# A graph layer on one core: the final gathers without iotas between them, the final part's first loads taken out of the final part, and one PSUM pool kept to the end

## The chip, the core and the metric

The kernel runs on one core of one Trainium2 chip. The core has five engines that work side by side, each through its own list of instructions in a fixed order: TensorE (PE, with its weight loads as PEld), VectorE (DVE), ScalarE (ACT), GpSimd (POOL) and SyncE (SP), which here only starts transfers. Data moves between memory and the core by DMA transfers, which an engine starts and which then run by themselves; an engine waits for another one, or for a transfer, by semaphores. The metric is the device time of one execution in microseconds (us); less is better.

## What is computed

The reference, cut to what matters (6,250 nodes, 100,000 edges sorted by `dst`, rows of 256 numbers):

```python
theta_x = (x[dst] - x[src]) @ theta_w.T + theta_b
phi_x = x[src] @ phi_w.T + phi_b
e = relu(theta_x + phi_x)
out = segment_max(e, dst, num_segments=6250)      # 0 where a node has no edge
return layernorm(x + where(isfinite(out), out, 0))
```

An edge's value is a part that hangs on `dst` alone, A = x theta^T + biases, plus a part that hangs on `src` alone, B = x (phi - theta)^T. So the maximum over a node's edges is relu(A of the node + the maximum of B over its sources), and the kernel looks for that maximum of B.

## The kernel before

**Stages.** The first 618 nodes ("the first part") are done by running maxima along sorted edges. The other 5,632 nodes are 44 tiles of 128. For these, B is cut into 17 slots of up to 383 rows. For each slot and node at most one source row is fetched, by a product with a one-hot matrix on PE (`slot_halves`, the matmuls of L1172; ACT and DVE make the one-hot tiles `hot` from row numbers `want`, which SP loads, L1207), and DVE takes the running maximum into `acc` (L1186). The edges that no slot has taken stand in a list of 257 steps, 256 of which are gathered: 33 groups of up to 8 steps, each step one indirect gather of 128 rows of `b_rows` on POOL (`gather_2`, L540) and one running maximum on DVE (L709). Each group's result is stored to `maxima_2` in memory (L1701; the last ones two steps at a time, L1748, and the last single step, L724). The slots' products and the list run side by side, from about 243 us to 605 us; this is called the list stage below.

**The final part** handles the 44 tiles in shares of 8, 8, 8, 4, 4, 4, 4, 2 and 2 tiles (`last_shares`, `rows_of`), and each share in pieces of two tiles (22 pieces). POOL gathers for each tile the rows of `maxima_2` that hold its nodes' list results (`gather` in `rows_of`, `g<-maxima,place`, 44 gathers; none can be issued before the last store of the list has landed). For a piece PE adds the bias (L1466), multiplies the transposed columns of x, `kept`, with theta (L1469), and transposes `acc` (L1478). DVE takes the maximum of gathered rows and `acc` (L1479), adds A (L1480), and adds relu of that to x with a sum along the row (L1483). Then comes the normalisation of the share, piecemeal between the next pieces: squares on ACT (L1512), the inverse root on DVE (L435 to L441), scaling on ACT (L1527; in the late shares half of it on DVE, L1523) and the store of the share by SP (L1533; the last by ACT, L1507).

**Rings and what they make wait.** x tiles (8 tiles of rows, 1 MB) stand in `x_ring` with 4 buffers; in the list stage the biases and the first part have used these. The transposed columns (4 tiles, 0.5 MB) stand in `kept_ring` with 3 buffers. Gathered rows have 6 buffers. A load into a used buffer waits for its last reader, which for an x tile is the store of the finished share.

**Order.** The program below is written in one order; a scheduler then lays down a fixed list for each engine, in which an instruction may be put ahead of others written before it if it is free to go. `behind_in_order` keeps an instruction behind a named one in that list. Before the change the x and `kept` loads of the final part are kept behind the last load of `want` in this way. SP's list is worked off strictly in order: an SP instruction that waits holds up all behind it.

**Iotas.** `gather` issues, while `paused[0]` is set, a small iota into a tile that nobody reads behind each gather (L508). It is set for a part of the first gathers and again for the final 44.

**PSUM.** 8 banks: `ps_misc` has two tiles of one bank, `ps_fetch` three of two banks (`ps_f`). In the final part a piece takes one bank for A and one for the transposed `acc`: at first by turns from `ps_misc` and from halves of `ps_f` (`by_turns`); once the last slot's work has been issued, `ps_fetch` is closed and a pool `ps_end` of six one-bank tiles (`ps_e`) opened in its place.

Of the kernel before, what the change touches and what calls it, by code (L numbers as in the profile page):

```python
# [39 lines left out]
FP = mybir.dt.float32  # L40
# [8 lines left out]
PSUM = bass.MemoryType.PSUM  # L49
DRAM = bass.MemoryType.DRAM  # L50

P = 128
BIG2 = 3.0e38
EPS = 1e-5
STEPS = 8
# [3 lines left out]
EARLY_SHARES = 12  # L59
# [19 lines left out]
RUNS_BEHIND = 3  # L79
# [3 lines left out]
X_AHEAD = 4  # L83
WANTS = 3
X_RING = 4
LAST_CHUNKS = 5
HALVES_AT_ONCE = 6
SPREAD_FROM = 9
# [5 lines left out]
LIST_GROUPS = (LIST + STEPS - 1) // STEPS  # L94
# [350 lines left out]
def gnn_kernel(ctx: ExitStack, tc: tile.TileContext, x, src, dst, theta_w, theta_b, phi_w, phi_b, out):  # L445
    nc = tc.nc
    N, D = x.shape
    E = src.shape[0]
    T = -(-E // P)
    KC = D // P  # L450
# [4 lines left out]
    NT1 = Q1 + 1  # L455
# [18 lines left out]
    body = ctx.enter_context(ExitStack())  # L474
# [3 lines left out]
    x_columns = dram.tile([P, TILES * KC * P], FP, name="x_columns")  # L478
# [19 lines left out]
    def node_rows(t, part, j0, n):  # L498
        if (part, j0, n) == LAST:
            return t[P * Q1 : N1, :].rearrange("p (o d) -> p o d", o=1)  # L500
        base, tiles = (0, Q1) if part == 1 else (N1, TILES)
        return flat(t, (base + j0) * D, [[tiles * D, P], [D, n], [1, D]])

    def present(t, part, j0, n):
        return t[: LEFT1 if (part, j0, n) == LAST else P, :n, :]
# [14 lines left out]
    def behind_in_order(one, name, reason):  # L520
        after = mybir.DependencyInfo(mybir.DependencyClass.NoSync, mybir.DependencyReason.DATA)
        tc.add_manual_dep(one.ins, name, after, reason=reason)
# [14 lines left out]
    paused = [False]  # L537
# [143 lines left out]
    one = nc.vector.tensor_copy(ids_1[:, : T1 + 2], dst_1)  # L681
# [740 lines left out]


    x_tiles, m_tiles = {}, {}
    def rows_of(part, j0, n, ps_tile):


        share = part, j0, n
        at = j0 % STEPS if part == 2 else 0
        if at == 0:  # L1430
            x_tiles[part] = x_ring.tile([P, STEPS, D], FP, name="x_f")
            rows = x_ring.tile([P, STEPS, D], FP, name="x_f") if part == 1 else gathered.tile([P, STEPS, D], FP, name="g")
            m_tiles[part] = rows
        x_f = x_tiles[part][:, at : at + n, :]
        if share == LAST:
            nc.vector.memset(x_f[:, 0, :], 0.0)
        one = nc.sync.dma_start(present(x_f, *share), node_rows(x, *share))
        if part == 2:
            behind_in_order(one, latest_codes[0], "chosen codes ahead of x")
        m = m_tiles[part][:, at : at + n, :]  # L1440
        maxima, places = (maxima_1, place_1) if part == 1 else (maxima_2, place_2)
        for k in range(n):
            gather(m[:, k, :], maxima, places[:, j0 + k : j0 + k + 1])
        totals = work.tile([P, STEPS], FP, name="totals", bufs=4)

        def piece(k):
            w = min(2, n - k)
            if part == 2:
                j = j0 + k
                if j % 4 == 0:  # L1450
                    x_tiles[0] = kept_ring.tile([P, 4 * KC, P], FP, name="kept")
                    rows = x_columns[:, j * KC * P : (j + 4) * KC * P]
                    one = nc.sync.dma_start(x_tiles[0], rows.rearrange("p (j n) -> p j n", n=P))
                    behind_in_order(one, latest_codes[0], "chosen codes ahead of the final rows")
                x_t = x_tiles[0][:, j % 4 * KC :]
            else:
                ps = ps_tile().rearrange("p (i n) -> p i n", i=4)
                for i in range(w):
                    for c in range(KC):
                        nc.tensor.transpose(ps[:, 2 * i + c, :], x_f[:, k + i, c * P : (c + 1) * P], ident)  # L1460
                x_t = work.tile([P, 4, P], FP, name="x_t")
                nc.scalar.copy(x_t[:, : 2 * w], ps[:, : 2 * w])
            yield
            a = ps_tile().rearrange("p (i d) -> p i d", i=2)
            bias_of = bias_terms.rearrange("p (o d) -> p o d", o=1)
            nc.tensor.matmul(a[:, :w, :], pick, bias_of.to_broadcast([P, w, D]), start=True, stop=False)  # L1466
            for i in range(w):
                for c in range(KC):
                    nc.tensor.matmul(  # L1469
                        a[:, i, :], x_t[:, 2 * i + c, :], weights[:, c, :], start=False, stop=(i == w - 1 and c == KC - 1)  # L1470
                    )
            some = m[:, k : k + w, :]
            if part == 2:
                ps = ps_tile().rearrange("p (i d) -> p i d", i=2)
                for i in range(w):
                    at = (j0 + k + i) * P
                    for c in range(KC):
                        nc.tensor.transpose(ps[:, i, c * P : (c + 1) * P], acc[:, c, at : at + P], ident)  # L1478
                nc.vector.tensor_tensor(some, some, ps[:, :w, :], op=ALU.max)  # L1479
            nc.vector.tensor_tensor(some, some, a[:, :w, :], op=ALU.add)  # L1480
            for i in range(k, k + w):
                y = x_f[:, i, :]
                one = nc.vector.scalar_tensor_tensor(  # L1483
                    y, m[:, i, :], 0.0, y, op0=ALU.max, op1=ALU.add, accum_out=totals[:, i : i + 1]
                )
                used.append(one.ins.name)
            yield

        return [piece(k) for k in range(0, n, 2)], normalise(part, j0, n, x_f, totals)
# [215 lines left out]
        while halves_left[0] > max(2 * LAST_CHUNKS, 2 * LAST_CHUNKS + halves_ahead * (1.0 - done)):  # L1705
            fetch_half()

    assert len(runs_left) == RUNS_BEHIND and RUNS_BEHIND + 1 + NT1 < EARLY_SHARES
    for i in range(LIST_GROUPS):
        if i == len(runs_left):  # L1710
            chunk_heads()
# [29 lines left out]
            add_up(n_bad, flags)  # L1741
        if i >= EARLY_SHARES:
            next(early_shares, None)
    next(heads, None)
    for i in range(LIST_GROUPS - LEAD, LIST_GROUPS - 1):
        for k in range(0, STEPS, 2):
# [5 lines left out]
    left = LIST - (LIST_GROUPS - 1) * STEPS  # L1752
    run(2, lists[-1], left, caps_2, (LIST_GROUPS - 1) * STEPS, carried_2t, (), carry_row)
    list_done[0] = latest_run[0]
    paused[0] = True
    for _ in range(HALVES_AT_ONCE):
        fetch_half()
    for _ in early_shares:
# [7 lines left out]
    def by_turns():  # L1766

        given[0] += 1
        if given[0] % 4 in (1, 2):
            return misc()  # L1770
        if not halves_of_tile:
            both = ps_fetch.tile([P, CW], FP, name="ps_f")
            halves_of_tile.extend([both[:, : 2 * D], both[:, 2 * D :]])
        return halves_of_tile.pop(0)

    fetch_open, pieces_done = [True], [0]

    def half_between():
        pieces_done[0] += 1
# [2 lines left out]

    at_end = Shares(by_turns)
    for share in last_shares:
        if not parts and begun[0] is None and fetch_open[0]:
            at_end.step()
            fetch_open[0] = False
            fetch.close()
            ps_end = body.enter_context(tc.tile_pool(name="ps_end", bufs=6, space=PSUM))
            at_end.ps_tile = lambda: ps_end.tile([P, 2 * D], FP, name="ps_e")  # L1790
        at_end.add(*share, between=half_between)
    assert not parts and not fetch_open[0]
    at_end.finish()


    body.close()
# [33 lines left out]
```

## Time and profile before

| | |
|---|---|
| median of 3 runs | 688.44 us (686.49 to 690.26) |
| the profiled execution's own time | 683.69 us |
| its span in the trace | 681.8 us |
| busy: PE / DVE / ACT / POOL | 633.4 / 623.5 / 491.3 / 471.8 us |
| share of the span | 93% / 91% / 72% / 69% |
| mean granted clock of PE | 0.981 |
| moved by DMA | 168.21 MB, 247 GB/s on average |

Shares over the whole span mix stages with different limits, so what the final part is worth is read from that part: which engine's or transfer's wait ends last there. A row of a timeline has a start (us from the start of the span), a length, the engine, the line of the kernel and the operation; in brackets stands how long the engine had been idle before and what ended that. Rows of SPq are starts of transfers by SP, not the transfers. The page gives the costs of the operations over the whole span as a mean; for single stages the timeline and tables by window are used.

### The profile page before, as it was taken

The numbers are of one execution on the slowest core, as the hardware profiler recorded it, in microseconds if no ns is written. First come the engines' busy times: TensorE is split into PE (matmuls) and PEld (weight loads), VectorE is DVE, ScalarE is ACT, GpSimd is POOL, SyncE is SP. The second block draws the span as 40 slices with busy tenths as digits, with TensorE's granted clock in tenths as the row PEclk, the third lists the DMA queues.
The fourth block names the chain that finished last, engine by engine and source line by source line (L and its number), as shares of the span: only waits on it lengthen the run. The fifth ranks groups of instructions, "written<-read, shape, count | busy, mean of one in ns | idle before, by whom it ended". The sixth has DMA issues, their size and how long they took to land.

```text
span 681.8 us, 9602 instructions
## 1 busy us (share of the span) xinstructions
PE 633.4 (93%) x2860; PEld 520.2 (76%) x2860; DVE 623.5 (91%) x1208; ACT 491.3 (72%) x678; POOL 471.8 (69%) x515
## 2 busy tenths in 40 slices
PE   4998889799999899999999999999999999998990
PEld 3887768687888688788888887888877777787880
DVE  6899999999999999999999999989998998767886
ACT  1554557989898577798696979786869786713775
POOL 7101288999992876777777777777777777468880
PEclk9999989999999899999999999999999999998995
DMA  7897644555655687778787989888788887895975
GB/s 238 304 340 282 224 127 138 149 169 189 208 171 189 201 279 263 256 231 270 239 297 220 305 289 272 271 262 271 255 266 283 266 285 261 279 365 178 321 262 193
DMA packets 61849, 168.21 MB, mean 247 GB/s; under 512 B 11926, under 2 KB 21950, under 8 KB 55774
## 3 DMA queue, kind: packets, MB, share of 16 engines
q1 hardware_dynamic: 40482, 107.92, 46.2%
q0 software_dynamic: 19040, 52.50, 26.3%
q10 hardware_dynamic: 2268, 7.11, 2.7%
q8 instruction: 24, 0.39, 0.2%
q14 instruction: 35, 0.29, 0.2%
HBM read 104.25 MB, written 63.23 MB: 246 GB/s over the span
## 4 chain that ended last, share of the span: by engine, by line
PE 40%; DVE 23%; DMA 16%; issue 10%; POOL 5%; ACT 4%; DVEq 0%; ACTq 0%; POOLq 0%; SPq 0%
PE ps_f L1172 34%; DMA g<-b_rows,list_src 8%; DVE acc L1186 4%; DVE g L709 4%; POOL g L540 4%; PE ps_b L793 3%; DMA want<-chosen_rows 2%; DVE hot L1219 2%; DMA g<-maxima,place 2%; DVE work L1354 2%; ACT hot L1221 1%; DMA out_dram<-x_f 1%; ACT x_f L1527 1%; DMA b_rows<-b_sb 1%; DVE g L1479 1%
## 5 line engine op out<-in xcount | busy, mean ns | idle before, releaser
L1172 PE MATMUL ps_f<-hot,terms 128*128 128x512 f32 x2112 | 491.5, 393 | 12.3 <-DVE acc L1186 10.2
L1172 PEld LDWEIGHTS ps_f<-hot,terms 128*128 128x128 f32 x2112 | 396.1, 189 | 101.2 <-DVE acc L1186 14.4
L540 POOL DMA_INDIRECT g<-b_rows,list_src x256 | 263.6, 1030 | 81.3 <-issue 46.8
L1221 ACT ACTIVATE hot<-want,minus_row 128x1024 fp32r<-128x1024 f16 (+1 forms) x201 | 207.9, 1070 | 77.9 <-PE ps_f L1172 76.1
L1186 DVE TENSOR_TENSOR acc<-acc,ps_f 128x1024 f32<-128x1024 f32 (+1 forms) x192 | 216.1, 1129 | 9.6 <-PE ps_f L1172 9.2
L1225 ACT ACTIVATE hot<-hot 128x1024 fp32r<-128x1024 f32 (+1 forms) x201 | 187.4, 974 | 0.9
L709 DVE SCALAR_TENSOR_TENSOR g<-g,caps 128x256 f32<-128x256 f32 x334 | 160.4, 483 | 15.3 <-DMA g<-b_rows,list_src 13.3
L540 POOL DMA_INDIRECT g<-b_rows,src x72 | 105.3, 1462 | 28.3 <-issue 14.4
L1219 DVE TENSOR_SCALAR hot<-want,row_id 128x1024 fp32r<-128x1024 f16 (+1 forms) x93 | 67.0, 724 | 3.5 <-DMA want<-chosen_rows 2.3
L793 PE MATMUL ps_b<-weights_b,x_t 128*128 128x256 f32 x228 | 53.2, 387 | 3.8 <-ACT x_t L781 3.5
L540 POOL DMA_INDIRECT g<-maxima,place x44 | 43.2, 982 | 17.9 <-DMA maxima<-g 10.9
L793 PEld LDWEIGHTS ps_b<-weights_b,x_t 128*128 128x128 f32 x228 | 42.9, 193 | 11.1 <-ACT x_t L781 5.6
L1512 ACT ACTIVATE squares<-x_f,r 128x256 bf16<-128x256 f32 x47 | 23.1, 493 | 19.5 <-DVE r L1509 19.5
L1469 PE MATMUL ps_e<-weights,kept 128*128 128x256 f32 x144 | 35.2, 388 | 0.0
L796 ACT COPY b_sb<-ps_b 128x512 f32<-128x512 f32 (+1 forms) x25 | 14.4, 577 | 24.8 <-PE ps_b L793 20.6
L1469 PEld LDWEIGHTS ps_e<-weights,kept 128*128 128x128 f32 x144 | 28.3, 197 | 4.0
L508 POOL IOTA pause<- 128x160 f32 x92 | 28.2, 306 | 0.6
L1527 ACT ACTIVATE x_f<-x_f,r 128x256 f32<-128x256 f32 x40 | 20.7, 587 | 10.5 <-DVE r L1519 10.5
L1003 POOL MEMSET work<- 128x1584 f32 x1 | 2.3, 2256 | 33.7 <-ACT b_sb L796 33.7
L781 ACT COPY x_t<-ps_xt 128x512 f32<-128x512 f32 (+1 forms) x29 | 16.2, 585 | 9.1 <-PE ps_xt L777 7.8
L1479 DVE TENSOR_TENSOR g<-g,ps_e 128x512 f32<-128x512 f32 x18 | 12.4, 688 | 7.4 <-DMA g<-maxima,place 3.3
L1184 ACT COPY acc<-ps_f 128x1024 f32<-128x1024 f32 (+1 forms) x12 | 11.2, 938 | 10.9 <-PE ps_f L1172 6.3
(288 smaller groups left out, 457.6 us busy)
## 6 DMA issues: line engine op xcount, KB each, us to landing
maxima<-g SPq DMA_DIRECT2D x41, 1024.0 KB
want<-chosen_rows SPq DMA_DIRECT2D x89, 256.0 KB
x_q<-in_x_dram SPq DMA_DIRECT2D x12, 512.0 KB
b_rows<-b_sb ACTq DMA_DIRECT2D x12, 512.0 KB
x_columns<-x_t SPq DMA_DIRECT2D x22, 256.0 KB
kept<-x_columns SPq DMA_DIRECT2D x11, 512.0 KB
raw<-b_rows SPq DMA_DIRECT2D x16, 256.0 KB
g<-b_rows,list_src POOLq DMA_INDIRECT x256, 5.0
```

The lines of the kernel that those rows point to most:

```text
L508: return nc.gpsimd.iota(t, pattern=[[step, t.shape[1]]], base=base, channel_multiplier=per_partition, allow_small_or_imprecise_dtypes=True,)
L540: one = nc.gpsimd.indirect_dma_start(out=to, out_offset=None, in_=table, in_offset=bass.IndirectOffsetOnAxis(ap=offsets, axis=0))
L709: one = nc.vector.scalar_tensor_tensor(g[:, k, :], last[part], caps[:, t : t + 1], g[:, k, :], op0=ALU.min, op1=ALU.max)
L793: nc.tensor.matmul(ps[:, h, :], x_t[:, h, k, :], weights_b[:, k, :], start=(k == 0), stop=(k == KC - 1))
L1172: one = nc.tensor.matmul(ps[:, w : w + 512], terms[:, part, b, h * P : (h + 1) * P], hot[b][:, w : w + 512], start=(i == 0), stop=(i == n ...
L1186: one = nc.vector.tensor_tensor(to, to, ps, op=ALU.max)
L1219: nc.vector.tensor_scalar(hot[b], want, row_id[:, b : b + 1], None, op0=ALU.is_equal)
L1221: one = nc.scalar.activation(hot[b], want, AF.Abs, bias=minus_row[:, b : b + 1], scale=1.0)
L1225: nc.scalar.activation(apart, apart.bitcast(FP), AF.Relu, bias=1.0, scale=-1.0)
L1469: nc.tensor.matmul(a[:, i, :], x_t[:, 2 * i + c, :], weights[:, c, :], start=False, stop=(i == w - 1 and c == KC - 1))
L1512: nc.scalar.activation(squares, x_f[:, k, :], AF.Square, bias=mean[:, k : k + 1], scale=1.0, accum_out=var[:, k : k + 1])
L1527: nc.scalar.activation(x_f[:, k, :], x_f[:, k, :], AF.Identity, bias=mean[:, k : k + 1], scale=inv[:, k : k + 1])
```

## The change

Three edits, all on the way from the list stage into the final part:

1. `paused[0] = True` ahead of the final part goes, so the 44 final gathers are issued with no iota behind them.
2. A new function `load_ahead` loads the first four x tiles (`X_TILES_AHEAD`) and the first three `kept` tiles (`KEPT_AHEAD`). It is written into the loop over the list groups, one call for each group from the 29th on (`AHEAD_FROM = 28`). These loads are not kept behind the loads of `want`. The final part takes these tiles instead of loading them.
3. `ps_fetch` is kept open to the end. Once no slot's work is left, `by_turns` gives two of eight tiles from `ps_misc` and six as halves of `ps_f`; `ps_end` is gone.

```diff
+X_TILES_AHEAD = 4
+KEPT_AHEAD = 3
+AHEAD_FROM = 28
...
+    def load_ahead(i):
+        if i < X_TILES_AHEAD:
+            x_f = x_ring.tile([P, STEPS, D], FP, name="x_f")
+            share = 2, i * STEPS, STEPS
+            nc.sync.dma_start(present(x_f, *share), node_rows(x, *share))
+            x_ahead.append(x_f)
+        if i < KEPT_AHEAD:
+            kept_ahead.append(load_kept(i * 4)[0])
+    def load_kept(j):
+        tile_of = kept_ring.tile([P, 4 * KC, P], FP, name="kept")
+        rows = x_columns[:, j * KC * P : (j + 4) * KC * P]
+        return tile_of, nc.sync.dma_start(tile_of, rows.rearrange("p (j n) -> p j n", n=P))
...
-            x_tiles[part] = x_ring.tile([P, STEPS, D], FP, name="x_f")
+            if part == 2 and x_ahead:
+                x_tiles[part] = x_ahead.pop(0)
+            else:
+                x_tiles[part] = x_ring.tile([P, STEPS, D], FP, name="x_f")
...
-        one = nc.sync.dma_start(present(x_f, *share), node_rows(x, *share))
-        if part == 2:
-            behind_in_order(one, latest_codes[0], "chosen codes ahead of x")
+        if part == 1 or j0 // STEPS >= X_TILES_AHEAD:
+            one = nc.sync.dma_start(present(x_f, *share), node_rows(x, *share))
+            if part == 2:
+                behind_in_order(one, latest_codes[0], "chosen codes ahead of x")
...
+        if i >= AHEAD_FROM:
+            load_ahead(i - AHEAD_FROM)
...
-    paused[0] = True
...
-        if given[0] % 4 in (1, 2):
+        every = 4 if halves_left[0] or begun[0] is not None else 8
+        if given[0] % every in (1, 2):
             return misc()
...
-        if not parts and begun[0] is None and fetch_open[0]:
-            at_end.step()
-            fetch_open[0] = False
-            fetch.close()
-            ps_end = body.enter_context(tc.tile_pool(name="ps_end", bufs=6, space=PSUM))
-            at_end.ps_tile = lambda: ps_end.tile([P, 2 * D], FP, name="ps_e")
         at_end.add(*share, between=half_between)
...
     at_end.finish()
+    fetch.close()
```

What stands in the lists of the engines now, at three places. (Line numbers of the changed kernel differ by some lines: L1207 is now L1210, L1701 is L1726, L1748 is L1775, L540 is L543, L1533 is L1558, and the loads ahead are L1435 for x and L1444 for `kept`.)

POOL, at the step from the list's gathers (from `b_rows`) to the final ones (from `maxima_2`, with the numbers of `place_2`), before:

```order
L540 DMA g<-b_rows,list_src 128x256 x112
L540 DMA g<-maxima_66,place_696 128x256
L508 IOTA pause 128x160
L540 DMA g<-maxima_66,place_696 128x256
L508 IOTA pause 128x160
```

And with the change, up to the read of the flag behind the kernel's main path:

```order
L543 DMA g<-b_rows,list_src 128x256 x40
L543 DMA x_f<-maxima_65,place_695 128x256 x4
L543 DMA g<-b_rows,list_src 128x256 x112
L543 DMA g<-maxima_66,place_696 128x256 x44
L1820 TENSOR_LOAD flags
```

The 44 iotas are gone and nothing has moved in their place.

SP, at the end of the list stage, before: the last load of row numbers, the last stores of the list, and four x tiles and three `kept` tiles between and behind these.

```order
L1207 DMA want<-chosen_rows 128x512
L1437 DMA x_f<-in_x_dram 128x2048
L1701 DMA maxima_66<-g 128x2048
L1748 DMA maxima_66<-g 128x512 x3
L1453 DMA kept<-x_columns 128x1024
L1748 DMA maxima_66<-g 128x512
L724 DMA maxima_66<-g 128x256
L1453 DMA kept<-x_columns 128x1024
L1437 DMA x_f<-in_x_dram 128x2048
L1453 DMA kept<-x_columns 128x1024
L1437 DMA x_f<-in_x_dram 128x2048
L1437 DMA x_f<-in_x_dram 128x1024 x2
```

With the change, at the same place:

```order
L1210 DMA want<-chosen_rows 128x512
L1726 DMA maxima_66<-g 128x2048
L1775 DMA maxima_66<-g 128x512 x4
L727 DMA maxima_66<-g 128x256
L1444 DMA kept<-x_columns 128x1024 x5
```

Only the list's stores are left there; the `kept` loads behind them are those of later pieces.

SP, earlier in the list stage, with the change: the store of the first part's four tiles, and the last of the four x tiles, which takes the buffer that this store reads.

```order
L1558 DMA out_dram<-x_f 128x1024
L1210 DMA want<-chosen_rows 128x1024
L1126 DMA raw<-b_rows 128x2x256
L1126 DMA raw<-b_rows 112x256
L1210 DMA want<-chosen_rows 128x1024
L1126 DMA raw<-b_rows 15x256
L1435 DMA x_f<-in_x_dram 128x2048
L1726 DMA maxima_66<-g 128x2048
```

Before, the same rows stand there without the x load. The other three x loads stand further ahead: two behind the store of the first part's last tile (which SP started at 423.57 us before), one ahead of a load of `want` that SP started at 482.86 us. The three `kept` loads stand behind the loads of the biases, at the start of the list stage (229 us before). So the scheduler has put all seven loads well ahead of the 29th group, each at the place where its buffer is free.

More of the change, by code (lines that the diff above doesn't have):

```diff
@@ L1424, in gnn_kernel @@
     x_tiles, m_tiles = {}, {}
+    x_ahead, kept_ahead = [], []
+    def load_ahead(i):
[10 more added lines that the diff above has]
+        return tile_of, nc.sync.dma_start(tile_of, rows.rearrange("p (j n) -> p j n", n=P))
     def rows_of(part, j0, n, ps_tile):
@@ L1449, in piece @@
                 j = j0 + k
[L1450 to L1453, printed above, removed]
+                if j % 4 == 0 and kept_ahead:
+                    x_tiles[0] = kept_ahead.pop(0)
+                elif j % 4 == 0:
+                    x_tiles[0], one = load_kept(j)
                     behind_in_order(one, latest_codes[0], "chosen codes ahead of the final rows")
@@ L1706, in halves_until @@
             fetch_half()
-    assert len(runs_left) == RUNS_BEHIND and RUNS_BEHIND + 1 + NT1 < EARLY_SHARES
+    assert AHEAD_FROM + X_TILES_AHEAD < LIST_GROUPS and len(runs_left) == RUNS_BEHIND and RUNS_BEHIND + 1 + NT1 < EARLY_SHARES
     for i in range(LIST_GROUPS):
@@ L1774, in by_turns @@
         return halves_of_tile.pop(0)
-    fetch_open, pieces_done = [True], [0]
+    pieces_done = [0]
     def half_between():
@@ L1784, in gnn_kernel @@
     for share in last_shares:
-        if not parts and begun[0] is None and fetch_open[0]:
-            at_end.step()
-            fetch_open[0] = False
-            fetch.close()
-            ps_end = body.enter_context(tc.tile_pool(name="ps_end", bufs=6, space=PSUM))
-            at_end.ps_tile = lambda: ps_end.tile([P, 2 * D], FP, name="ps_e")
         at_end.add(*share, between=half_between)
-    assert not parts and not fetch_open[0]
+    assert not parts and begun[0] is None
     at_end.finish()
+    fetch.close()
     body.close()
```

## The prediction

> **What bounds the kernel now.** I read the table by windows first, then the chain of waits, then the timelines of POOL, PE, DVE and SP around the end of the list stage. The table's columns are the window, its length, the busy time (and instructions) of PE, PEld, DVE, ACT and POOL, PE's granted clock, the DMA engines' busy share, and GB/s.
>
> ```profile
> 520.00:530.00 10.00, 9.54 (x43) 7.57 (x42) 9.69 (x14) 9.96 (x12) 7.78 (x8) 1.00 0.86 294
> 530.00:540.00 10.00, 10.00 (x46) 8.14 (x45) 9.65 (x16) 5.35 (x7) 7.73 (x8) 1.00 0.99 312
> 590.00:600.00 10.00, 9.40 (x42) 7.28 (x41) 8.24 (x13) 6.30 (x9) 0.03 (x1) 1.00 0.95 332
> 600.00:610.00 10.00, 10.00 (x51) 8.51 (x50) 5.18 (x6) 0.48 (x1) 8.03 (x13) 1.00 1.00 381
> 640.00:650.00 10.00, 10.00 (x56) 8.74 (x55) 8.21 (x27) 8.68 (x27) 8.82 (x15) 1.00 1.00 364
> 660.00:670.00 10.00, 3.96 (x22) 3.21 (x21) 9.19 (x38) 9.71 (x32) 3.56 (x6) 0.82 0.59 211
> ```
>
> No engine is idle for long in the final part, so busy shares don't decide. The chain does (start, length, what):
>
> ```profile
> 589.09 5.89 DMA g<-b_rows,list_src
> ...
> 597.29 2.85 DMA maxima<-g
> ...
> 662.43 6.11 DMA g<-maxima,place
> ```
>
> It runs from the list's last gather (589.09) through its landing and the list's last store to the final gathers, and near its end through the landing of the last of these. Between these two points POOL never rests:
>
> ```profile
> 589.09 0.95 POOL L540 DMA_INDIRECT g<-b_rows,list_src  x1 [0.30 <-issue]
> 600.97 0.95 POOL L540 DMA_INDIRECT g<-maxima,place  x1 [10.93 <-DMA maxima<-g]
> 601.92 0.28 POOL L508 IOTA pause<- 128x160 f32 x1
> 602.37 0.96 POOL L540 DMA_INDIRECT g<-maxima,place  x1 [0.16 <-issue]
> ...
> 662.43 1.18 POOL L540 DMA_INDIRECT g<-maxima,place  x1 [0.16 <-issue]
> ```
>
> So 44 gathers start from 600.97 to 662.43, 61.46 / 43 = 1.43 us apart, 2.86 us for a piece. The last one lands at 662.43 + 6.11 = 668.54, and from there to the end of the span are 681.8 - 668.54 = 13.3 us. DVE's rows show that it meets late rows on the way (the maximum with the gathered rows, L1479, opens each piece; pieces 1, 6, 13, 14, 16 and 22):
>
> ```profile
> 608.97 0.69 DVE L1479 TENSOR_TENSOR g<-g,ps 128x512 f32<-128x512 f32 x1 [2.70 <-DMA g<-maxima,place]
> ...
> 625.51 0.69 DVE L1479 TENSOR_TENSOR g<-g,ps_e 128x512 f32<-128x512 f32 x1
> ...
> 642.88 0.69 DVE L1479 TENSOR_TENSOR g<-g,ps_e 128x512 f32<-128x512 f32 x1
> 646.58 0.69 DVE L1479 TENSOR_TENSOR g<-g,ps_e 128x512 f32<-128x512 f32 x1 [1.48 <-DMA g<-maxima,place]
> ...
> 653.04 0.69 DVE L1479 TENSOR_TENSOR g<-g,ps_e 128x512 f32<-128x512 f32 x1 [1.79 <-DMA g<-maxima,place]
> ...
> 668.66 0.69 DVE L1479 TENSOR_TENSOR g<-g,ps_e 128x512 f32<-128x512 f32 x1 [0.66 <-PEq L1799]
> ```
>
> (The name behind the last wait is PE's sequencer, which had no work left; the gather landed 0.12 us before.) From piece 6 to piece 13, 625.51 to 642.88, DVE takes 17.37 / 7 = 2.48 us for each, and more behind them: POOL's 2.86 us is the slowest of the paces, but not by much.
>
> **The iotas.** An iota costs 0.28 us, but a gather behind a gather is not issued at once either. The list's gathers have no iotas, and the row of all of them from 469 us on (count, ns least/median/most, first and last start), with the landing times there, is the nearest measure:
>
> ```profile
> L540 POOL DMA_INDIRECT g<-b_rows,list_src x92: 942/947/1538, 469.3 to 589.1; - x92
> DMA to landing us min/median/max: 2.8/4.9/7.4
> ```
>
> 91 steps in 119.8 us are 1.316 us each, since 0.30 us of idle replaces 0.28 + 0.16 and some gathers are long. The term is 43 x (1.43 - 1.316) = 4.9 us, not 44 x 0.28 = 12. Bounds: 0, if the idle time grows to what the iota took; 43 x (1.43 - 0.95 - 0.30) = 7.7, if every gather takes the shortest.
>
> **The loads.** At the end of the list SP now starts, among the list's stores, these loads:
>
> ```profile
> 583.44 0.92 SPq L1437 DMA_DIRECT2D x_f<-in_x_dram  x1
> ...
> 594.61 0.43 SPq L1453 DMA_DIRECT2D kept<-x_columns  x1
> ...
> 597.68 0.42 SPq L1453 DMA_DIRECT2D kept<-x_columns  x1
> 598.20 0.41 SPq L1437 DMA_DIRECT2D x_f<-in_x_dram  x1
> 598.65 0.48 SPq L1453 DMA_DIRECT2D kept<-x_columns  x1
> 599.32 1.85 SPq L1437 DMA_DIRECT2D x_f<-in_x_dram  x3
> ```
>
> That is 4 MB of x and 1.5 MB of `kept`, and the DMA engines are 0.95 to 1.00 busy there. The list's last gather took 5.89 us to land; 4.9 is the median of the 92. Without the loads I take the median: 1.0 us, after which the list's last store and the first final gather move up. Bounds 0 and 5.89 - 2.8 = 3.1. For the store's 2.85 us and the last final gather's 6.11 us (beside stores of the output, which stay) I take no change. For one gather of 128 KB alone, the Trainium skill's "DMA: Bandwidth & Descriptors" (section "Anatomy of one DMA — SWDGE (gpsimd) path") gives about 2.0 us plus the bytes at 436 GB/s, so an estimate of 2.3 us, by which this term would be 3.6 and the sum below 8.5. The trace's shortest landing, 2.8 us, nearly agrees, but its median is twice that.
>
> In their new places the loads run beside the list's gathers and PE's products, whose one-hots need `want` loads. SP would wait at the last x load for the store of the first part's rows:
>
> ```profile
> 524.10 2.08 SPq L1533 DMA_DIRECT2D out_dram<-x_f  x1
> 526.26 0.54 SPq L1207 DMA_DIRECT2D want<-chosen_rows  x1
> ...
> 529.82 0.37 SPq L1207 DMA_DIRECT2D want<-chosen_rows  x1
> 530.24 0.44 SPq L1123 DMA_DIRECT2D raw<-b_rows  x1
> 533.54 0.32 SPq L1701 DMA_DIRECT2D maxima<-g  x1
> 534.14 0.32 SPq L1207 DMA_DIRECT2D want<-chosen_rows  x1
> ```
>
> Behind it stand a store of the list and the next `want`. The gap to 533.54 hides up to 2.9 us of such a wait, and three `want` buffers lie ahead of PE. What the loads could cost surely is POOL: a gather beside full DMA engines lasts up to 1538 ns instead of 947, and one such for each of four x loads is 2.4 us. In 530 to 540 us, at 0.99 busy, POOL still issued its 8 gathers in the window, as in the one ahead of it at 0.86. So I take 0, with bounds 0 and a loss of 2.4; what covers it is that the list's end hangs on POOL's pace alone, and PE's products have 2.5 us to spare (next).
>
> **The PSUM edit and PE.** With `ps_end`, PE waits for everything in `ps_f` to be read, and runs cold after it:
>
> ```profile
> 605.38 1.89 PE L1469 MATMUL ps<-weights,kept 128*128 128x256 f32 x8
> ...
> 618.99 0.76 PE L1466 MATMUL ps_e<-bias_terms,pick 128*128 128x512 f32 x1 [2.72 <-DVE g L1480]
> 619.55 3.09 PE L1469 MATMUL ps_e<-weights,kept 128*128 128x256 f32 x8
> ...
> 663.37 0.60 PE L1478 MATMUL ps_e<-ident,acc 128*128 128x128 f32 x4
> ```
>
> That is 2.72 us, and 3.09 - 1.89 = 1.2 us. Eight banks by turns let PE run four pieces ahead, where DVE's first reads come at 609 us; I take both as gone, so PE ends at 663.97 - 3.9 = 660.1. It is worth nothing by itself, since the last piece's rows land later: 668.54 - 4.9 - 1.0 = 662.6. DVE starts at 607.8 (when PE's first piece is done) and at 2.48 us a piece reaches the 22nd at 607.8 + 21 x 2.48 = 659.9. Both stay 2.5 us and more under 662.6, so the gathers still come last, and the tail of 13.3 us behind them stays.
>
> **Sum.** 4.9 + 1.0 + 0 + 0 = 5.9 us. The profiled execution took 683.69 us (span 681.8), so it would take 677.8. It lies 4.75 us under the median of 688.44 shown, and below all three of its runs, so I subtract the 5.9 from the median: **682.5 us**, 0.9% less. What a measurement of this kernel can tell from no change is about 0.5%, 3.4 us.
>
> **Rivals.**
>
> *PE and DVE take over.* If gathers step at 1.25 us and land sooner, the last rows are there before PE's 660.1 and DVE's 659.9; the gain ends at 668.54 - 660.1 = 8.4 us: 680.0. For it: most list gathers take 947 ns. Against it: the long ones, and DMA engines 1.00 busy in 640 to 650 us. Chance 0.17.
>
> *DVE holds the pace.* From 646.58 to 668.66 a piece took 22.08 / 8 = 2.76 us, since the normalisations of the late, small shares fall there. If that is DVE's own pace throughout, the last piece starts at 607.8 + 21 x 2.76 = 665.8, a gain of 2.9: 685.5. For it: DVE busy 9.19 of 10 us in 660 to 670. Against it: its waits for rows of 1.48 and 1.79 us in that stretch. Chance 0.12.
>
> *The change doesn't do what it says.* The iota may only have filled the time that a gather needs before the next; then the pace stays, and the 1.0 us of the loads is all: 687.4. Against it: 0.30 us is what the list's rows show. Chance 0.08.
>
> *Slower: the loads cost the list stage more than the final part gains.* 4 MB of x now move while the DMA engines are 0.86 to 0.99 busy. If each MB at about 300 GB/s (294 and 312 in the windows) pushes back what is queued with it by 3.5 us, and this adds up, with 3.2 us more if the store started at 526.18 takes the 7.74 us of a later 1 MB store and SP waits until 533.9 instead of 530.7, the list's end moves by 17.2 us and the time by 17.2 - 5.9 = 11.3: 699.7. That store's row:
>
> ```profile
> 645.39 7.74 DMA out_dram<-x_f
> ```
>
> It decides from 9.3 us on (5.9 + 3.4). Against it: POOL's pace hardly falls at 0.99 busy. The Trainium skill's "DMA: Bandwidth & Descriptors", section "Queues, rings and completion order", speaks for it: an engine goes round its queues packet by packet, so that a gather beside a large load has to share each DMA engine with it; by that, landings and not only starts get later, as the list's last gather of 5.89 us beside the x load agrees. Chance 0.08.
>
> **Chances and range.** My forecast has 0.55. Faster by over 0.5%: 0.55 + 0.17 = 0.72; within: 0.12 + 0.08 = 0.20; slower: 0.08. The range leaves out the slow rival and the far side of two others: from 677.0 (680.0 where PE and DVE take over, less 3 us, since the runs shown lie 3.8 us apart and the median of three can be off by most of that) to 687.0, just under the 687.4 of a pace that stays.
>
> **What would show it.** Right: final gathers 1.3 us apart, the first near 600 us and the last near 656, no wait of PE at the fifth piece, PE's end near 660, and the same 13 us behind the last landing. Wrong: final gathers over 1.4 apart; a last list gather later than 590 us, or DVE or PE waiting for `want` or the list's rows between 430 and 540 us; DVE without idle time from 608 us on and a tail longer than 13 us.

## The result, and the profile after

| | before | after |
|---|---|---|
| median, first comparison | 688.1 us (686.49 to 690.26, 4 runs) | 678.03 us (675.47 to 682.79, 4 runs) |
| ratio | | 0.9842 (95% interval 0.9804 to 0.9881) |
| profiled execution / its span | 683.69 / 681.8 us | 682.79 / 681.0 us |

The change made the kernel 1.6% faster in the comparison that the prediction was made for. That isn't the whole result. (The median of 688.44 shown ahead is that of three of the four runs of before.) In the experiments, on four chips, the kernel before took 784 to 795 us, and on the two of them where the same change was run (1 and 9) it made the kernel slower, 1.018 and 1.021. Both are taken up below, the first comparison first. Some executions of a kernel come out a per cent or more slower than its others; a median counts them and a ratio doesn't, so a ratio can differ a little from the quotient of two medians. Line numbers are now those of the changed kernel, as in the section on the change.

The two profiled executions differ by only 0.9 us, because the one of after is the longest of its four runs and that of before is shorter than all of its runs. So they are compared stage by stage. POOL's rows for the gathers (count, ns least/median/most, first and last start), of the kernel before and of the changed one:

```profile
L540 POOL DMA_INDIRECT g<-b_rows,list_src x256: 942/947/2287, 234.6 to 589.1; - x128
L540 POOL DMA_INDIRECT g<-maxima,place x44: 947/960/1184, 601.0 to 662.4; - x44
```

```profile
L543 POOL DMA_INDIRECT g<-b_rows,list_src x256: 945/950/2283, 240.0 to 595.6; - x128
L543 POOL DMA_INDIRECT g<-maxima,place x44: 945/949/1071, 605.2 to 659.5; - x44
```

The list begins 5.4 us later. That isn't put down to the change: over all the traces of this case the list begins anywhere from 234.6 to 243.3 us, and the changed kernel on chip 1 begins it at 234.8. It takes 355.6 us from first to last gather instead of 354.5. Then come the gains, in POOL's timeline of after:

```profile
595.57 1.17 POOL L543 DMA_INDIRECT g<-b_rows,list_src  x1 [0.30 <-issue]
605.22 1.02 POOL L543 DMA_INDIRECT g<-maxima,place  x1 [8.49 <-DMA maxima<-g]
606.54 0.95 POOL L543 DMA_INDIRECT g<-maxima,place  x1 [0.30 <-issue]
...
659.49 0.94 POOL L543 DMA_INDIRECT g<-maxima,place  x1 [0.30 <-issue]
```

The first final gather comes 605.22 - 595.57 = 9.65 us behind the last one of the list, where it was 11.88: 2.2 us won. The 44 take 54.27 us where they took 61.46: 7.2 us won; they are 54.27 / 43 = 1.26 us apart. From the last one to the end of the span it is 21.5 us, where it was 19.4: 2.1 us given back. Together that is 7.3 us behind the last list gather, less 1.1 us in the list: 6.2 us. Those, the 5.4 us late start and the spans' 0.8 us agree.

What is given back has a name. DVE's last two pieces in after (start, length, operation, idle time ahead of it), and PE's last row:

```profile
664.86 0.69 DVE L1504 TENSOR_TENSOR g<-g,ps 128x512 f32<-128x512 f32 x1 [0.30 <-DMA g<-maxima,place]
...
667.38 0.69 DVE L1504 TENSOR_TENSOR g<-g,ps_f 128x512 f32<-128x512 f32 x1
```

```profile
665.28 0.60 PE L1503 MATMUL ps_f<-ident,acc 128*128 128x128 f32 x4
```

The last maximum has no wait in front of it: its rows were there, and it comes 1.5 us behind PE's end at 665.88. The last gather landed 3.2 us after its start, at 662.7, which is 4.6 us ahead of the last maximum. So the last gather no longer ends last; DVE does, with PE close ahead of it. The chain of waits still names a gather,

```profile
655.73 8.86 DMA g<-maxima,place
```

and so does the wait of 0.30 us in front of the piece at 664.86, the last but one. This is a misreading by the view and not a late gather. This gather landed 4.0 us after its start, at 659.7, and no landing below took more than 6.9 us; what the view takes for its end is an update of its semaphore at 664.58 that no transfer made. PE's sums for that piece were ready at 663.5, so what held DVE for the 0.30 us isn't shown. The landing times from 600 us on, before and after (each trace has them for 22 of the 44 gathers):

```profile
DMA to landing us min/median/max: 2.7/4.9/7.3
```

```profile
DMA to landing us min/median/max: 2.7/3.4/6.9
```

The table by windows, of after, has the way there (window, length, busy time of PE, PEld, DVE, ACT, POOL, granted clock, DMA share, GB/s):

```profile
610.00:620.00 10.00, 10.00 (x52) 8.52 (x51) 7.24 (x16) 0.00 (x0) 7.56 (x9) 1.00 0.51 156
...
630.00:640.00 10.00, 10.00 (x56) 8.74 (x55) 9.62 (x33) 6.85 (x20) 7.56 (x9) 1.00 0.76 218
640.00:650.00 10.00, 10.00 (x55) 8.77 (x54) 9.39 (x35) 6.74 (x20) 7.56 (x9) 1.00 0.96 347
650.00:660.00 10.00, 10.00 (x55) 8.75 (x54) 9.25 (x44) 8.90 (x34) 7.55 (x9) 1.00 0.97 370
```

PE has no gap from 610 us to its end, so the stop at the fifth piece is gone, and DVE is 92 to 96% busy from 630 us on. From 625 us to its last maximum DVE's longer waits add up to 1.3 us, 1.0 of them for ACT's squares. The moved loads can be seen in the list stage, in the waits from 240 to 600 us (total, times, longest), after and before:

```profile
DVE hot L1222 <- DMA want<-chosen_rows: 7.4, 5, 2.7
...
DVE g L712 <- DMA g<-b_rows,list_src: 6.7, 5, 3.1
```

```profile
DVE g L709 <- DMA g<-b_rows,list_src: 13.3, 15, 2.6
...
DVE hot L1219 <- DMA want<-chosen_rows: 1.1, 1, 1.1
```

DVE waits 6.3 us more for `want` and 6.6 us less for the list's rows.

### The profile page after: what moved, and what is told of

The parts are those of the page before. It is cut to its first block, busy times and chain, and to the rows that moved or that the text cites. A ratio compares the mean times of both kernels' runs of the same rounds, so it can differ in the third digit from the quotient of the medians.

```text
span 681.0 us, 9560 instructions
## 1 busy us (share of the span) xinstructions
PE 633.3 (93%) x2860; PEld 521.0 (77%) x2860; DVE 623.8 (92%) x1208; ACT 491.6 (72%) x678; POOL 455.9 (67%) x471
## 4 chain that ended last, share of the span: by engine, by line
PE 47%; DMA 15%; POOL 13%; DVE 12%; issue 7%; ACT 4%; SPq 0%; DVEq 0%; POOLq 0%; ACTq 0%
PE ps_f L1175 38%; POOL g L543 12%; DMA want<-chosen_rows 7%; PE ps_b L796 5%; DVE acc L1189 3%; DVE g L712 2%; DMA g<-b_rows,list_src 2%; ACT hot L1224 1%; DMA g<-maxima,place 1%; DVE work L1357 1%; DMA src_w<-in_src_dram,window 1%; POOL pause L511 1%; DMA x_columns<-x_t 1%; DVE x_f L1508 1%; DVE g L1504 1%
## 5 line engine op out<-in xcount | busy, mean ns | idle before, releaser
L543 POOL DMA_INDIRECT g<-b_rows,list_src x256 | 267.0, 1043 | 79.5 <-issue 47.7
L543 POOL DMA_INDIRECT g<-b_rows,src x72 | 100.4, 1395 | 28.5 <-issue 14.7
L1222 DVE TENSOR_SCALAR hot<-want,row_id 128x1024 fp32r<-128x1024 f16 (+1 forms) x93 | 67.2, 726 | 14.4 <-DMA want<-chosen_rows 11.8
L796 PE MATMUL ps_b<-weights_b,x_t 128*128 128x256 f32 x228 | 55.3, 398 | 7.2 <-ACT x_t L784 6.9
L543 POOL DMA_INDIRECT g<-maxima,place x44 | 42.1, 957 | 21.6 <-issue 11.9
L799 ACT COPY b_sb<-ps_b 128x512 f32<-128x512 f32 (+1 forms) x25 | 14.4, 577 | 27.2 <-PE ps_b L796 23.3
L1494 PE MATMUL ps_f<-weights,kept 128*128 128x256 f32 x128 | 30.2, 379 | 0.0
L1494 PEld LDWEIGHTS ps_f<-weights,kept 128*128 128x128 f32 x128 | 24.3, 190 | 3.2
L1357 DVE COPY_PREDICATED work<-words,work 128x316 int32<-128x316 int32 (+9 forms) x11 | 18.4, 1672 | 0.0
L1508 DVE SCALAR_TENSOR_TENSOR x_f<-g,x_f 128x256 f32<-128x256 f32 x44 | 17.3, 427 | 0.5
```

The costliest lines, as they stand in the source:

```text
L543: one = nc.gpsimd.indirect_dma_start(out=to, out_offset=None, in_=table, in_offset=bass.IndirectOffsetOnAxis(ap=offsets, axis=0))
L796: nc.tensor.matmul(ps[:, h, :], x_t[:, h, k, :], weights_b[:, k, :], start=(k == 0), stop=(k == KC - 1))
L1222: nc.vector.tensor_scalar(hot[b], want, row_id[:, b : b + 1], None, op0=ALU.is_equal)
L1357: one = nc.vector.copy_predicated(done[:, :n], moves[:, :n], done[:, shift : shift + n])
L1494: nc.tensor.matmul(a[:, i, :], x_t[:, 2 * i + c, :], weights[:, c, :], start=False, stop=(i == w - 1 and c == KC - 1))
L1508: one = nc.vector.scalar_tensor_tensor(y, m[:, i, :], 0.0, y, op0=ALU.max, op1=ALU.add, accum_out=totals[:, i : i + 1])
```

## The experiments

They ran in five groups, each beside runs of the kernel before on the same chip. No result of the first comparison says which chip it used. Ratios are given with their 95% intervals.

**The edits one by one (chip 1; before: 795.36 us).** The iotas alone:

```diff
-    paused[0] = True
```

> The kernel before with the first edit alone: no iotas behind the 44 final gathers; loads and PSUM pools as before. Theory A (the gathers' pace sets the end of the final part): final gathers 1.26 to 1.32 us apart instead of 1.43, the last one's start 5 to 7 us nearer to the first, time 4 to 7 us less (ratio 0.990 to 0.994). Rival B (PE's stop at the pool swap and DVE set the end, the iotas only fill the time): the same pace change, but 0 to 2 us of time, PE still stops about 2.7 us at the fifth piece and DVE's waits for gathered rows vanish.

Measured: 811.28 us, 1.0197 (1.0148 to 1.0245). Slower, which no theory had.

The loads alone (the change's second edit, with the iotas and `ps_end` kept):

> The kernel before with the second edit alone: four x tiles and three tiles of transposed columns loaded ahead; iotas and the pool swap as before. Theory A: the list's last gather lands in about 5 us instead of 5.9, the first final gather is issued 1 to 2 us sooner behind the list's last gather, and the time falls by 0 to 2 us (ratio 0.997 to 1.000). Rival C (the loads cost the list stage): PE or DVE wait for row numbers or list rows between 430 and 550 us by 2 us or more in all, and the time is the same or up to 5 us more.

Measured: 793.89 us, 0.9982 (0.9945 to 1.0019): within what theory A gave, and not told from no change.

PSUM alone:

```diff
-        if given[0] % 4 in (1, 2):
+        every = 4 if halves_left[0] or begun[0] is not None else 8
+        if given[0] % every in (1, 2):
...
-            fetch.close()
-            ps_end = body.enter_context(tc.tile_pool(name="ps_end", bufs=6, space=PSUM))
```

> The kernel before with the third edit alone: the fetch pool stays open to the end. Theory A: PE's stop of 2.7 us at the fifth piece and the cold matmuls behind it go, PE ends 3 to 4 us sooner, but the gathers come last as before: 0 to 1 us of time (ratio 0.998 to 1.000). Rival B (PE's stop sets the end): 3 to 4 us less (ratio 0.994 to 0.996).

Measured: 795.8 us, 0.9969 (0.9927 to 1.001), which doesn't decide between A and B.

The changed kernel as it is:

> The changed kernel once more, beside the three single edits on one chip, for the size of the whole and a second trace. Theory A: 6 to 10 us less than before (ratio 0.985 to 0.991), the final part from PE's last slot product to the end of the span about 68 us instead of 76. Rival D (the 10 us of the first comparison hold a difference between runs in the stages that the change doesn't touch): 5 to 6 us less.

Measured: 808.59 us, 1.0182 (1.0131 to 1.0233). So here the iotas are what the whole change turns on, and their removal costs 2%. The change's own trace on this chip shows how. (The execution traced took 796.4 us, the shortest of its six: beside the trace of the loads alone its list is 14.3 us shorter, 415.4 against 429.7, and its final part 14.4 us longer, 122.0 against 107.6.) First by windows, in the final part:

```profile
660.00:680.00 20.00, 20.00 (x90) 16.57 (x89) 15.01 (x23) 12.13 (x14) 5.69 (x6) 1.00 0.42 151
680.00:700.00 20.00, 8.21 (x44) 6.84 (x42) 5.12 (x10) 0.00 (x0) 15.35 (x16) 0.79 0.43 130
700.00:720.00 20.00, 8.02 (x20) 5.48 (x20) 1.56 (x6) 0.00 (x0) 15.12 (x17) 0.59 0.36 106
720.00:740.00 20.00, 8.65 (x24) 5.83 (x24) 5.27 (x15) 0.88 (x3) 5.78 (x7) 0.52 0.26 78
740.00:760.00 20.00, 20.00 (x109) 17.51 (x108) 18.83 (x68) 13.17 (x46) 0.00 (x0) 1.00 0.61 211
```

From about 688 to 734 us PE, DVE and ACT all but stand still, but for some 5 us of PE's work from 700.3 us on, while POOL issues gathers at its full pace. The DMA engines are at most 0.43 busy, so they aren't full. PE's granted clock is low (0.52 to 0.79) only in the windows in which PE mostly waits. POOL's last gather starts at 726.66, and from 734.5 us on everything runs again. In DVE's and PE's timelines:

```profile
685.03 0.42 DVE L1508 SCALAR_TENSOR_TENSOR x_f<-g,x_f 128x256 f32<-128x256 f32 x1
...
698.77 0.69 DVE L1504 TENSOR_TENSOR g<-g,ps_f 128x512 f32<-128x512 f32 x1 [13.32 <-remote]
...
714.87 0.69 DVE L1189 TENSOR_TENSOR acc<-acc,ps_f 128x512 f32<-128x512 f32 x1 [14.69 <-remote]
```

```profile
705.40 0.38 PE L1494 MATMUL ps<-weights,kept 128*128 128x256 f32 x1
708.56 0.58 PE L1494 MATMUL ps<-weights,kept 128*128 128x256 f32 x1 [2.78 <-issue]
710.67 0.58 PE L1494 MATMUL ps<-weights,kept 128*128 128x256 f32 x1 [1.53 <-issue]
713.46 0.59 PE L1494 MATMUL ps<-weights,kept 128*128 128x256 f32 x1 [2.21 <-issue]
...
735.05 3.61 PE L1494 MATMUL ps_f<-weights,kept 128*128 128x256 f32 x8
```

"Remote" is a release that the trace can't name; "issue" is no wait that it shows. PE's rows matter most: eight matmuls of one sum, with nothing to wait for between them, start 2.1 to 3.5 us apart, and behind POOL's last gather eight of them take 3.61 us together. So it isn't only rows that land late. Nor is it the clock: one such matmul takes 0.38 us ahead of the stop and 0.58 us in it, which is little beside the 2.1 to 3.5 us.

This gave a new theory, E: on these chips gathers that come 1.25 us apart hold the other engines up, and the iota, idle work on POOL, leaves them room.

**The edits in pairs, and a longer pause (chip 9; before: 794.5 us).** All but the iota edit (`paused[0] = True` put back):

> The change without its first edit: the 44 iotas stay behind the final gathers, the loads are moved and the PSUM pool is kept. Two chips have been seen, one on which the kernel before takes about 688 us and one on which it takes about 795. On the first: theory A (the spacing of the gathers sets the end) gives only the loads' term of the prediction, 1.0 us, so about 687, a ratio of 0.998 to 1.000, with final gathers 1.4 us apart and the end still set by the last gather's landing; if it gives 0.99 or less, the loads and the PSUM pool are worth more than the prediction says and the iotas less. Rival B (the stop of PE at the fifth piece and DVE set the end) gives the gain of nearly 10 us here, with the iotas in place. Rival C (loads cost the list stage) gives 1.002 or more. On the second chip, where taking the iotas away cost 2%, theory E (there the other engines are held up while the gathers come with no iota between them) gives no change, 0.995 to 1.002.

Measured: 793.41 us, 0.9951 (0.991 to 0.9992), at the low end of what theory E gave.

All but the loads (the iotas' and the PSUM edit on the kernel before):

> The change without its second edit: no iotas and the PSUM pool kept, but the loads of the final part where they were. On the first chip (before: about 688): theory A gives the iotas' term, 4.9 us, a ratio of 0.993, and with the loads beside the first gathers again their landing is late (DVE waits for gathered rows more than 2 us in the final part). Theory F (PE and DVE have taken over in the changed kernel, and the loads were needed for that) gives the same 0.993 and a PE or DVE that waits for x or kept; if the ratio is 0.985, the loads give nothing. On the second chip theory E gives the loss of the iota edit alone, 1.015 to 1.025.

Measured: 814.59 us, 1.0258 (1.0211 to 1.0305), a little more than expected.

Two iotas behind each final gather, in the changed kernel:

```diff
         if paused[0]:
-            in_turn(iota(pause, 1, 0, 0))
+            for _ in range(pauses[0]):
+                in_turn(iota(pause, 1, 0, 0))
...
+    paused[0], pauses[0] = True, 2
```

> The changed kernel with two iotas behind each of the final gathers instead of none. On the first chip theory A says that the gathers set the end once they are slower than PE and DVE: 1.25 us plus twice about 0.29 us makes 1.7 us a gather, 44 times 1.7 is 75 us from a first gather near 605, so a last landing near 685 and a time of about 699, a ratio near 1.015. Rival: if the end isn't set by the gathers' spacing at all, the time stays near 678, a ratio near 0.985. On the second chip theory E says that a longer pause frees the other engines: the time falls below that of the kernel with one iota, a ratio of 0.98 to 0.995; if spacing is not what holds them up, the ratio is that of the changed kernel, 1.018, or higher by the longer stretch of the gathers.

Measured: 781.28 us, 0.9822 (0.9778 to 0.9865). POOL does more for nothing, and the kernel is the faster for it, as E said. The windows, against those above:

```profile
680.00:700.00 20.00, 20.00 (x94) 16.77 (x93) 14.10 (x24) 6.69 (x8) 12.98 (x25) 1.00 0.32 102
700.00:720.00 20.00, 20.00 (x110) 17.44 (x110) 16.25 (x51) 9.06 (x28) 17.15 (x35) 1.00 0.55 170
```

From 720 to 760 us PE is less busy here too (15.50 and 14.21 of 20 us), but each wait of PE has a name, DVE. The waits of PE in the final part that the traces give as "issue" come to 14.7 to 29.0 us in the four runs that have neither iotas nor a wait there (the iotas alone, the changed kernel on chips 1 and 9, all but the loads), to 0.5 us with one iota (the loads alone) and to none with two. With one iota DVE still waits 20.3 us for a release that the trace can't name.

**Fewer gathers under way, and iotas in the list (chip 2; before: 792.33 us).** The changed kernel with a wait instead of iotas:

```diff
-            gather(m[:, k, :], maxima, places[:, j0 + k : j0 + k + 1])
+            gather(m[:, k, :], maxima, places[:, j0 + k : j0 + k + 1], used[k - STEPS] if part == 2 and j0 else None)
```

> The changed kernel, without iotas, but from the ninth tile on each final gather waits for the sum into x of a tile some eight to ten ahead of it, so that few gathers are under way that nobody has used yet. On the chip where the kernel before takes about 795: theory E2 (it is the number of gathers under way that holds the other engines up) gives no long stall, 765 to 782, a ratio of 0.96 to 0.985. Theory E1 (it is the spacing of 1.25 us itself) gives a stall in the first ten gathers and again whenever they come back to back, 790 to 805, a ratio of 0.99 to 1.015. If nothing of the stall goes, 1.018. On the chip where it takes about 688 the gathers come ten tiles ahead of their use, 12 us against a landing of 4.9, so the time of the changed kernel stays, 675 to 683, a ratio of 0.98 to 0.99.

Measured: 780.05 us, 0.9827 (0.9778 to 0.9877). The time is as E2 (the number under way) had it, but the trace shows stalls as E1 (the spacing) had them, one behind each run of gathers that come back to back. POOL, then DVE:

```profile
721.39 0.94 POOL L543 DMA_INDIRECT g<-maxima,place  x1 [2.20 <-DVE x_f L1508]
...
732.62 0.94 POOL L543 DMA_INDIRECT g<-maxima,place  x1 [0.30 <-issue]
737.95 0.94 POOL L543 DMA_INDIRECT g<-maxima,place  x1 [4.39 <-DVE x_f L1508]
```

```profile
728.78 0.69 DVE L1504 TENSOR_TENSOR g<-g,ps 128x512 f32<-128x512 f32 x1
735.80 0.69 DVE L1504 TENSOR_TENSOR g<-g,ps_f 128x512 f32<-128x512 f32 x1 [4.80 <-remote]
```

Ten gathers 1.25 us apart, then POOL has to wait, and about 2 us after that DVE goes on. The wait doesn't take the stall away, it cuts it short. So the two readings can't be told apart by the time alone.

One iota behind each of the list's gathers too, in the kernel with two iotas behind the final ones:

```diff
     list_carry()
-    paused[0] = False
+    paused[0] = True
```

> Two iotas behind each final gather, and one behind each of the 256 gathers of the list too. On the chip of about 795: theory E says that the list stage, which is some 65 us longer there, is held up by the same thing, so it shortens: from the kernel with two iotas (781) to 720 to 770, a ratio of 0.91 to 0.97. If the list stage is long for another reason, the ratio is 0.98 or more, and up to 256 times 0.16, 41 us, more. On the chip of about 688, where POOL's gathers set the pace of the list, it is 1.03 or more.

Measured: 744.76 us, 0.9421 (0.9356 to 0.9485). POOL's rows of the run with the wait, whose list stage has no iotas, on the same chip, then of this one:

```profile
L543 POOL DMA_INDIRECT g<-b_rows,list_src x256: 940/947/1952, 241.7 to 672.1; - x128
L543 POOL DMA_INDIRECT g<-maxima,place x44: 941/946/1148, 694.3 to 761.3; - x44
```

```profile
L543 POOL DMA_INDIRECT g<-b_rows,list_src x256: 948/956/2095, 237.2 to 637.4; - x128
L543 POOL DMA_INDIRECT g<-maxima,place x44: 947/952/1206, 645.6 to 721.7; - x44
```

Each list gather costs POOL more, and the list takes 400.2 us instead of 430.4. From its last gather to the first final one it is 8.2 us instead of 22.2. The final part takes 95.1 us to the end of the span (740.7), as with the same two iotas on chip 9 (685.2 to 780.9, 95.7).

**Putting them together.** Iotas in the list, none in the final part, and the wait there (chip 0; before: 784.04 us):

> One iota behind each gather of the list, none behind the final ones, and the final ones from the ninth tile on wait for the sum into x of a tile eight to ten ahead. On the chip of about 795, if the two remedies add up: from the first final gather to the end the trace had 95 us with two iotas and 90 with the wait, so 5 us off the 745 of the run with iotas in the list, 735 to 745, a ratio of 0.93 to 0.94. If the wait frees the engines only because the list stage had left work over, 745 to 755. On the chip of about 688 the iotas in the list cost up to 0.16 us times 256, 41 us, where POOL's gathers set the pace of the list, so 700 to 720, a ratio of 1.02 to 1.05; a ratio below 1 there would say that the list isn't paced by POOL.

Measured: 738.57 us, 0.9412 (0.935 to 0.9475). In the trace the final part takes 89.7 us (645.2 to 734.9), 5.4 us less than with two iotas, as expected. That the two gains add up in the time isn't shown: the time lies in the range given, but on this chip the kernel before is 8 us faster too, and the ratio beside it is nearly that of the run on chip 2 with iotas in the list and two behind the final gathers (0.9421).

One iota behind every gather, and the wait (chip 9; before: 794.25 us):

> One iota behind each gather of the list and each final one, and the wait of the run before. Where the kernel before takes 784 to 795: if the spacing holds the engines up whatever the number under way, the iota behind the final gathers still helps, 3 to 8 us below the run without it, a ratio of 0.93 to 0.937. If the wait alone already frees them, the iotas only make the final gathers later, a ratio of 0.94 to 0.95. Where it takes about 688: 1.02 to 1.05.

Measured: 741.72 us, 0.933 (0.9261 to 0.9399). The interval overlaps that of the run before it, and in the two profiled executions the final part isn't shorter (92.3 us against 89.7), so whether the iota adds something to the wait stays open. It is 6.7% faster than the kernel before and, on the same chip, 8.5% faster than the changed one.

The changed kernel once more, in the same group:

> The changed kernel itself once more. The first comparison of it, in which the kernel before took 688, gave a ratio of 0.984; the experiments so far, in which it took 784 to 795 on each chip, gave 1.018 for it. If that is a matter of one chip, this one can give either; if it goes with the time of the kernel before, a ratio of 1.015 to 1.025 where that is 784 or more, and 0.98 to 0.99 where it is about 688.

Measured: 810.72 us, 1.0214 (1.0157 to 1.0271). So it isn't one chip's doing.

What the final part takes, from the first final gather to the end of the span, in the profiled executions:

| behind a final gather | final part |
|---|---|
| an iota, first comparison (before) | 80.8 us |
| nothing, first comparison (after) | 75.8 us |
| nothing, experiments (iotas alone / changed kernel on chips 1 and 9 / all but the loads) | 125.0 / 122.0 / 122.0 / 121.9 us |
| one iota, experiments (loads alone) | 107.6 us |
| two iotas, experiments | 95.7 us |
| nothing, but the wait, experiments | 89.8 us |

## Why the prediction was right, and where it wasn't

**The side and the size.** It said 682.5 us, 5.9 us off; the medians are 10.1 us apart, the traces 6.2 us by stages. The 6.2 lies below what the interval allows (8.2 to 13.5 us), and one execution of each kernel can't say where the other 4 us are. None of the experiments met the conditions of the first comparison again, so for it the shares of the edits rest on its two traces alone. That 678.0 us lies within the range (677.0 to 687.0) is in part luck: its low end was set by the first rival, the traces account for 6.2 us only, and on the two chips where the change was run again it cost 2%.

**The iotas' term (4.9 us).** The mechanism was right and the size too small: 7.2 us, spacing 1.26 us where 1.316 was taken, near the bound of 7.7. The list gathers' mean, on which the term rested, holds long gathers (1538 ns at most); of the final ones none took over 1071. The prediction put the long ones down to full DMA engines. The traces don't bear that out: over the list before, the 85 gathers of more than 1 us stood beside DMA engines 0.81 busy on average, the other 171 beside 0.85, and from 640 to 660 us, at 0.96 and 0.97, all final gathers but one (1.06 us) took 0.95 us. What makes a gather long stays open.

**The loads' term (1.0 us).** Also right and too small: the way from the last list gather to the first final one got 2.2 us shorter, inside the bounds. Of that, 1.2 us lie ahead of the start of the list's last store (8.20 us behind the last list gather before, 6.97 after), which is the term; the other 1.0 us lies behind it, where the prediction took no change. The landing taken for the last final gather, 6.11 us, got shorter too, to 3.2: the median of the landings is 3.4 us, where it was 4.9. By the rule of the Trainium skill's "DMA: Bandwidth & Descriptors", section "Anatomy of one DMA — SWDGE (gpsimd) path", the estimate for one alone is 2.3 us; with the loads out of the way the trace's median comes nearer to that, and still lies 1.1 us above it.

**Nothing for the list stage.** It cost 1.1 us between the first and last gather, within the 2.4 taken as a bound. `want` did come late, as the prediction said would speak against it, but the list's rows came earlier by as much. The rival of 11 us isn't there.

**The gathers still come last: this step failed.** Counted from the last list gather, PE's end was forecast at 71.0 us and came at 70.3; DVE's last piece at 70.8 and came at 71.8; the last rows' landing at 73.5 and came, 3.2 us behind the last issue, at 67.1. PE and DVE were sized well, the gathers ran 6 us ahead of the forecast, and so the end passed to PE and DVE, the first rival's state. The tail behind the start of the last piece, 13.6 us, is close to the 13.3 of the forecast; behind the last landing it is 18.3 us, a tail longer than 13 us, which the prediction named as a sign against it. That is why 9.4 us on POOL's path became 7.3.

**What the prediction didn't have.** Its slower rival was the loads. It weighed the iota only as time that POOL loses, never as time in which other engines get on. In the experiments that is what counts: 2% slower without, 2% faster with two. The trace before spoke against it: there 92 list gathers without iotas stood 1.316 us apart beside a PE that was busy nearly throughout. On the other chips the same list stage has it already. The changed kernel from 300 to 400 us, in the first comparison and on chip 1:

```profile
300.00:400.00 100.00, 99.99 (x444) 82.23 (x443) 92.08 (x151) 82.79 (x102) 77.72 (x73) 1.00 0.83 264
```

```profile
300.00:400.00 100.00, 87.86 (x361) 69.67 (x360) 75.13 (x123) 67.98 (x91) 65.51 (x64) 0.95 0.67 213
```

PE loses 12 us of these 100, and DVE 17.

## What to carry to other kernels

An instruction that does nothing may be there for what it keeps apart. Before it goes, ask who else runs while it does, and measure with none, one and two of them, on more than one chip: the order of the three times tells whether it is a cost or a cover. Where an edit takes time from the one path that ends last, work out when the next engine ends; here 9.4 us won on the gathers were worth 7.3.

## What the runs showed of the hardware

- The same kernel took 688 us in the first comparison and 784 to 795 us on each of the four chips of the experiments (0, 1, 2 and 9). Up to the list's first gather both are alike (234.6 us in the kernel before, 234.8 us in the changed one on chip 1); the difference begins where gathers come 1.25 us apart: from 250 to 260 us, just behind the list's first gathers, PE is busy for 10.00 of 10 us in the changed kernel of the first comparison, for 0.00 on chip 1, and again for 10.00 on chip 2 with an iota behind each list gather. It isn't that transfers take longer: from 300 to 400 us a packet of the queue of POOL's gathers takes 0.147 us on average on chip 1 (2977 packets, 27.4% of 16 engines' 100 us) and 0.151 us in the first comparison (3461 packets, 32.6%). What is different about the chips or their setting isn't recorded, and stays open.
- In these experiments, spaced 1.25 us apart, gathers of 128 rows of 1 KB hold PE, DVE and ACT up, at a DMA share of at most 0.43 (chip 1, 680 to 740 us); with two iotas (44 in 76.5 us, 1.78 us apart) PE runs at 20.00 of 20 us from 680 to 720 us. Through which part of the chip isn't shown. The Trainium skill's "Runtime: NRT & Kernel Launch", section "Instruction fetch mechanics", says that engines fetch instructions by DMA in blocks of 256. By that, a late fetch would stop PE once in a block and not between one matmul and the next, so PE's rows above speak against it. The trace on chip 1 has three fetches of instructions from 680 to 734 us, of 1.30, 0.31 and 0.43 us, so the fetches that it shows aren't long either. The Trainium skill's "DMA: Bandwidth & Descriptors" guesses, in the section "Latency and other measured facts", that the rings of such transfers slow two of the sixteen DMA engines. No run here shows the engines one by one, and late transfers alone wouldn't explain PE's rows either.
- A pause on POOL behind each list gather shortened the list by 30 us on chip 2, although by the prediction's rows (0.28 + 0.16 for an iota instead of 0.30 of idle time) 256 of them add up to 36 us of POOL's time.
